# A macaron block on one core: PSUM as four pairs of banks instead of two double and four single places

## The chip, the cores and the metric

The kernel runs on one core of one Trainium2 chip. The metric is device time in microseconds (us) of one execution. A core has five engines with instruction queues of their own: TensorE (PE) multiplies matrices and writes only to PSUM; VectorE (DVE) and ScalarE (ACT) read PSUM and compute on rows; GpSimd (POOL) computes on SBUF alone; SyncE (SP) issues transfers. Each queue is worked off in order, and engines wait for each other through semaphores. PSUM has eight banks of 128 partitions by 512 fp32 values. One matmul writes into one bank.

## The reference

The input is x, 32 sequences of 256 tokens by 128 channels, in fp32. Three residual steps follow each other:

```
x = x + 0.5 * ffn(layernorm(x))          # weights L0_ffn_*
x = x + channel_attention(layernorm(x))  # weights L0_attn_W*
x = x + 0.5 * ffn(layernorm(x))          # the same weights as the first
```

`ffn` is a small transformer of two layers. Each layer shifts half of the channels by one token, projects to q, k and v for 8 heads of 64, normalizes q and k to length one, applies a scaled rotary embedding, and attends within windows of 64 tokens, looking back one window:

```
q, k, v = split(shift_token(x) @ wqkv, 3)
q, k = rotary_xpos(l2norm(q) * qs, l2norm(k) * ksc)
x = x + local_attention(q, k, v) @ wo
h = layernorm(shift_token(x)) * lg + lb
a, g = split(h @ w1 + b1, 2)
x = x + (a * gelu(g)) @ w2 + b2
```

`channel_attention` attends over channels instead of tokens, with 16 heads of 8 channels, so its score matrix is 128 by 128 for a sequence.

## The kernel before, in words

A sequence is two tiles of 128 tokens. For each of the 32 sequences the program builds a list of steps: load (SP), `ffn`, `channel_attention`, `ffn`, store. A step is a `plan.op`: the engines that may run it, a cost in us written out by hand, the function that emits its instructions, the steps it comes after, and the places it uses. A place is a buffer that a step takes from a list of a kind ("hT", "qk", "pT" and so on in SBUF) and gives back when its last user is done.

PSUM has two kinds of places: two "wide" ones of two banks each, and four "bank" ones of one bank (lines 112 and 113). Wide places hold the q and k projection (`project`, L197, two matmuls of 512 columns), the scores (`scores`, mask at L247 and 32 small products at L255) and the attended values (`attended`, L289, 32 small products). Bank places hold everything else: the value projection (L231), transposes of four or two 128-column blocks (`transposed`, L140, and `shifted_T`, L178), the output projection (L312), the hidden layer in three chunks (L381), its second matrix (L414) and the products of the channel attention (L458, L470, L496). Whatever lies in PSUM is read by ACT or DVE: copies (`evac`, L130, ACT unless DVE would end more than 1 us earlier), squares (L203), rotary products (L205 and L208), maximum and difference of the scores (L261 and L264), division (L296 and L297), GELU (L389), gated product (L396) and the residual sums (L317, L422, L501). GpSimd adds and scales q and k (L222 and L225), and computes the inverse norms (L124).

The order of all engines' work is fixed when the program is built. `Plan.order` simulates the engines with the costs of the steps, for up to eight sequences in flight. `begin` gives the earliest start of a step: when its inputs are there, its engine is free and each kind it lacks has a place, at the time at which that place was given back, plus a few hundredths of a us for a semaphore. `choose` picks the engine, `go` issues the step that can begin first, and takes the place that was given back longest ago. Every 15 TensorE steps the planner tries 16 orders of the next 60, with random delays, and keeps the one that ends first on TensorE. Its result is the order in which the steps' functions are called.

The framework below it then derives the semaphore waits from this order and from the tiles and slices that each instruction reads and writes. The planner does not see them.

Of the kernel before, what the change touches and what calls it, by code (L numbers as in the profile page):

```python
# [8 lines left out]
F32 = mybir.dt.float32  # L9
# [6 lines left out]
P = 128  # L16
# [24 lines left out]
def kernel(ctx: ExitStack, tc: tile.TileContext, ins: dict, out: bass.AP):  # L41
# [6 lines left out]
    psum = ctx.enter_context(tc.tile_pool(name="psum", bufs=2, space=PSUM))  # L48
# [30 lines left out]
    plan = Plan()  # L79

    for kind, n, shape in (
# [27 lines left out]
        ("v1", 12, [P, NT]),  # L109
    ):  # L110
        plan.places(kind, [hold.tile(shape, F32, name=f"{kind}{i}") for i in range(n)])
    for kind, n, shape in (("wide", 2, [P, 2, 512]), ("bank", 4, [P, 512])):
        plan.places(kind, [psum.tile(shape, F32, tag=f"{kind}{i}", name=f"ps_{kind}{i}", bufs=1) for i in range(n)])
    plan.places("sequence", range(CHAINS))

    for t in plan.free["vt"]:
# [531 lines left out]
class Plan:  # L648
# [16 lines left out]
    class Place:  # L665
        def __init__(self, kind):
            self.kind, self.t, self.users = kind, None, 0
# [2 lines left out]
        pass  # L670

    def __init__(self):
        self.free, self.ops, self.rank, self.base = {}, [], 0, 0

    def places(self, kind, tiles):
        self.free[kind] = list(tiles)
# [81 lines left out]
    def lacks(self, o):  # L758
# [4 lines left out]
                need[p.kind] = need.get(p.kind, 0) + 1  # L763
        return need

    def begin(self, o, engine):

        t = max(o.given[engine], self.clock[engine], self.clock["POOL"] if o.apart else 0.0)
        sync = self.SYNC[engine]
        for p in o.uses:  # L770
            if p.last and p.last[1] != engine and p.kind in self.TURNS:
                t = max(t, p.last[0] + sync)
        for k, n in self.lacks(o).items():
            if len(self.room[k]) < n:
                return None
            t = max(t, (min(self.since[k]) if n == 1 else sorted(self.since[k])[n - 1]) + sync)
        return t

    def choose(self, o):


        choice = None
        for engine, us in zip(o.engines, o.us):
            t = self.begin(o, engine)
            if t is None:
                return None
            load = self.TABLE * (engine == "ACT" and o.table not in (None, self.table))
            end = t + us + load + (self.RATHER if engine != o.engines[0] else 0.0)
            if choice is None or end < choice[0]:
                choice = (end, engine, t, us + load, t + load)  # L790
        return choice[1:]

    def go(self, until, later, chance):


        import heapq

        heap, barred = [], {}

        def push(o, t):  # L800
            heapq.heappush(heap, (round((t + later[o]) / self.ALIKE), o.key, o))

        def enter(o):
            if o not in later:
                later[o] = chance()
            push(o, min(o.given.values()))

        for o in self.ready:
            enter(o)
        while heap and (until is None or self.through < until):  # L810
            first, _, o = heapq.heappop(heap)
            choice = self.choose(o)
            if choice is None:
                barred.setdefault(next(k for k, n in self.lacks(o).items() if len(self.room[k]) < n), []).append(o)
                continue

            engine, t, us, rank = choice
            if round((rank + later[o]) / self.ALIKE) > first:
                push(o, rank)
                continue  # L820
            taken = []
            for p in o.uses:
                self.undo.append((p, dict(p.__dict__)))
                if p.t is None:
                    i = min(range(len(self.room[p.kind])), key=lambda i: self.since[p.kind][i])
                    p.t = self.room[p.kind].pop(i)
                    self.since[p.kind].pop(i)
                    taken.append((p, p.t))
                    for d in barred.pop(p.kind, []):
                        enter(d)  # L830
            self.out.append((o, engine, taken))
            self.clock[engine] = t + us
            if o.apart:
                self.clock["POOL"] = t + us
            self.through += engine == "PE"
            self.undo.append((o, {"done": None}))
            o.done = (t + us + o.late + self.TAIL[engine], engine)
            if engine == "ACT" and o.table not in (None, self.table):
                self.table = o.table
                waiting = [h[2] for h in heap]  # L840
                heap.clear()
                for d in waiting:
                    enter(d)
            for p in o.uses:
                p.left -= 1
                p.end, p.last = max(p.end, o.done[0]), o.done
                if not p.left:
                    self.room[p.kind].append(p.t)
                    self.since[p.kind].append(p.end)
                    for d in barred.pop(p.kind, []):  # L850
                        enter(d)
            for d in o.then:
                self.undo.append((d, {"wait": d.wait}))
                d.wait -= 1
                if not d.wait:
                    d.given = {
                        e: max(x.done[0] + (self.SYNC[e] if x.done[1] != e or x.late else 0.03) for x in d.after)
                        for e in d.engines
                    }
                    enter(d)  # L860
        self.ready = [h[2] for h in heap] + [o for os in barred.values() for o in os]
        return bool(heap) or not self.ready
# [48 lines left out]
```

## Time and profile before

| | |
|---|---|
| median of 3 runs | 2841.89 us (2840.95 to 2842.41) |
| the profiled execution's own time | 2842.17 us |
| its span, from the first instruction to the last | 2840.1 us |
| TensorE matmuls (PE) | 2788.2 us busy, 98% |
| TensorE weight loads (PEld) | 2114.4 us, 74% |
| VectorE (DVE) | 2135.1 us, 75% |
| ScalarE (ACT) | 1993.7 us, 70% |
| GpSimd (POOL) | 2302.2 us, 81% |
| granted TensorE clock, mean | 0.997 |

A group of instructions in the profile is one line, engine, operation and tile; after the bar stand its busy time in us, the mean time of one in ns, and the idle time of its engine just before it with what ended most of it. A line of the waits reads: engine, tile and line that waited, what ended the wait, us in total, number of waits, the longest. In the timeline stand start and length in us. A busy PE is not a PE at its peak: records of matmuls overlap, and their ends are modelled. Helpers share lines: every PSUM copy is L130, every transpose through `transposed` L140.

### The profile page before, as it was taken

How to read it: one execution, taken by the hardware profiler on the slowest of the kernel's cores; microseconds unless marked ns; L12 is line 12 of the kernel's file. 1: busy time of each engine (PE TensorE's matmuls, PEld its weight loads, DVE VectorE, ACT ScalarE, POOL GpSimd, SP SyncE). 2: the span in 40 equal slices, each digit the busy share in tenths (PEclk: the TensorE clock that was granted, in tenths of full speed). 3: DMA queues.
4: the chain of work that ended last, by engine and by line, in shares of the span. 5: the costliest groups of instructions: out<-in, count | busy, mean ns of one | idle time of the engine just before them, and what ended most of it. 6: DMA issues, size and time to landing. Idle time of an engine off the chain costs nothing.

```text
span 2840.1 us, 106723 instructions
## 1 busy us (share of the span) xinstructions
PE 2788.2 (98%) x46200; PEld 2114.4 (74%) x46200; DVE 2135.1 (75%) x3764; ACT 1993.7 (70%) x3601; POOL 2302.2 (81%) x2098
## 2 busy tenths in 40 slices
PE   7999999999999999999999999999999999999999
PEld 4777777777777777777777777777777777777677
DVE  5778778778777778677777777877787777777776
ACT  4776776767677776767777776776767677776675
POOL 8988879698889778787798878878788788875975
PEclk9999999999999999999999999999999999999999
DMA  3111121111211111111112112111121111110211
GB/s 109 31 46 44 38 52 47 39 51 37 55 38 47 46 40 48 38 49 45 44 51 53 46 36 52 46 36 47 47 55 47 37 46 44 43 46 20 53 42 41
DMA packets 125726, 129.82 MB, mean 46 GB/s; under 512 B 56606, under 2 KB 75592, under 8 KB 125256
## 3 DMA queue, kind: packets, MB, share of 16 engines
q1 hardware_dynamic: 124440, 122.60, 16.5%
q8 instruction: 363, 5.95, 0.9%
q14 instruction: 107, 0.88, 0.1%
q10 hardware_dynamic: 816, 0.39, 0.0%
HBM read 8.13 MB, written 4.19 MB: 4 GB/s over the span
## 4 chain that ended last, share of the span: by engine, by line
PE 86%; DVE 6%; ACT 3%; POOL 3%; issue 1%; DMA 1%; SPq 0%; ACTq 0%; DVEq 0%; POOLq 0%
PE ps_bank L140 20%; PE ps_wide L197 14%; PE ps_bank L381 11%; PE ps_wide L289 9%; PE ps_bank L312 8%; PE ps_wide L255 7%; PE ps_bank L231 7%; PE ps_bank L414 6%; PE ps_wide L247 3%; PE ps_bank L458 1%; PE ps_bank L178 1%; DVE qk L205 1%; DVE sq L208 1%; ACT sq L203 1%; POOL rn L124 1%
## 5 line engine op out<-in xcount | busy, mean ns | idle before, releaser
L124 POOL TENSOR_TENSOR rn<-ssq,mhalf 128x16 f32<-128x16 f32 x256 | 748.3, 2923 | 21.3
L222 POOL TENSOR_TENSOR qk<-qk,sq 128x1024 f32<-128x1024 f32 x256 | 606.4, 2370 | 163.8 <-DVE sq L208 83.4
L225 POOL TENSOR_TENSOR qk<-qk,rn 128x1024 f32<-128x1024 f32 x256 | 487.7, 1908 | 10.4
L197 PE MATMUL ps_wide<-wqkv,hT 128*128 128x512 f32 x1024 | 489.2, 600 | 2.0 <-ACT hT L130 1.2
L205 DVE TENSOR_TENSOR qk<-ps_wide,tab 128x1024 f32<-128x1024 f32 x256 | 312.2, 1219 | 184.7 <-ACT sq L203 101.7
L381 PE MATMUL ps_bank<-zT,w 128*128 128x256 f32 (+1 forms) x1536 | 379.3, 383 | 2.8 <-DVE zT L130 1.7
L203 ACT ACTIVATE sq<-ps_wide 128x1024 f32<-128x1024 f32 x256 | 262.5, 1025 | 154.2 <-PE ps_wide L197 91.6
L208 DVE TENSOR_TENSOR sq<-ps_wide,tab 128x1024 f32<-128x1024 f32 x256 | 311.4, 1217 | 66.8 <-ACT sq L203 32.6
L130 ACT COPY pT<-ps_bank 96x512 f32<-96x512 f32 x505 | 283.3, 584 | 101.1 <-PE ps_bank L140 98.7
L214 DVE TENSOR_REDUCE ssq<-sq 128x16 f32<-128x1024 f32 x256 | 310.0, 1211 | 57.2 <-ACT sq L203 56.4
L381 PEld LDWEIGHTS ps_bank<-zT,w 128*128 128x128 f32 (+1 forms) x1536 | 257.8, 178 | 70.8 <-issue 15.0
L140 PE MATMUL ps_bank<-ident,pr 128*96 128x128 f32 x2048 | 290.2, 275 | 5.1 <-ACT pr L267 2.4
L140 PE MATMUL ps_bank<-ident,qk 128*128 128x128 f32 x2048 | 290.8, 276 | 3.1 <-POOL qk L225 2.4
L261 DVE TENSOR_REDUCE mx<-ps_wide 128x8 f32<-128x768 f32 x256 | 242.9, 949 | 62.8 <-PE ps_wide L255 61.7
L197 PEld LDWEIGHTS ps_wide<-wqkv,hT 128*128 128x128 f32 x1024 | 179.4, 191 | 145.7 <-issue 133.3
L289 PE MATMUL ps_wide<-vt,pT 96*32 96x65 f32 x8192 | 282.1, 221 | 3.5 <-ACT pT L130 1.4
L289 PE MATMUL ps_wide<-vm,pT 96*32 96x65 f32 x8192 | 283.9, 221 | 1.5 <-DVE sq L208 0.7
L312 PE MATMUL ps_bank<-wo,oT 128*128 128x128 f32 x2048 | 275.9, 279 | 2.7 <-ACT oT L130 1.0
L140 PEld LDWEIGHTS ps_bank<-ident,qk 128*128 128x128 f32 x2048 | 236.4, 141 | 48.1 <-issue 24.0
L312 PEld LDWEIGHTS ps_bank<-wo,oT 128*128 128x128 f32 x2048 | 251.2, 191 | 27.1 <-issue 10.3
L140 PEld LDWEIGHTS ps_bank<-ident,pr 128*96 128x96 f32 x2048 | 225.1, 126 | 60.7 <-issue 29.3
L289 PEld LDWEIGHTS ps_wide<-vt,pT 96*32 96x32 f32 x8192 | 240.6, 109 | 37.8 <-issue 17.6
(101 smaller groups left out, 5430.1 us busy)
## 6 DMA issues: line engine op xcount, KB each, us to landing
vm<-vt SPq DMA_DIRECT2D x256, 195.0 KB
vm<-vt SPq DMA_DIRECT2D x256, 130.0 KB
vm<-vt SPq DMA_DIRECT2D x256, 65.0 KB
y<-y SPq DMA_DIRECT2D x128, 56.0 KB
x<-in_x SPq DMA_DIRECT2D x32, 128.0 KB
out<-x SPq DMA_DIRECT2D x32, 128.0 KB
y<-y SPq DMA_DIRECT2D x128, 7.5 KB
y<-y SPq DMA_DIRECT2D x128, 0.2 KB
```

The costliest lines, as they stand in the source:

```text
L124: nc.gpsimd.tensor_tensor(dst, src, mhalf[:, :n], ALU.pow)
L140: nc.tensor.transpose(pt.t[:rows, j * P : (j + 1) * P], src, ident)
L197: nc.tensor.matmul(wide.t[:, a], lhsT(), wqkv[:, l, a * INNER : (a + 1) * INNER], start=True, stop=True)
L203: "ACT", 0.92, lambda e: nc.scalar.activation(sq.t, pq(), AF.Square), [m], [wide, sq]
L205: c = plan.op("DVE", 1.14, lambda e: nc.vector.tensor_mul(qk.t, pq(), cos), [m] + made["tables"][l], [wide, qk])
L208: lambda e: nc.vector.tensor_mul(sn.t.rearrange(five, x=2), pq().rearrange(five, x=2)[:, :, :, ::-1, :], sin.rearrange(five, x=2)),
L214: "DVE", 1.13, lambda e: nc.vector.tensor_reduce(ssq.t, sq.t, AX.X, ALU.add), [s], [sq, ssq]
L222: f = plan.op("POOL", 2.42, lambda e: nc.gpsimd.tensor_add(qk.t, qk.t, sn.t), [c, i], [qk, sn])
L225: lambda e: nc.gpsimd.tensor_mul(qk.t, qk.t, rn.t.unsqueeze(3).to_broadcast([P, 2, HEADS, DH])),
L289: nc.tensor.matmul(o()[q, r, j, :], pTs[r].t[:FR, j, q], v[:, 2 * j + r, :], start=True, stop=True)
L312: nc.tensor.matmul(pw.t[:, :P], oT.t[:, j, :], wo[:, l, j, :], start=j == 0, stop=j == PAIRS - 1)
L381: nc.tensor.matmul(pa.t[:w, i * SEQ : (i + 1) * SEQ], w1[:, l, i * HID + c0 : i * HID + c0 + w], zf(), start=True, stop=True,)
```

## The change

The two kinds of PSUM places become one pool. There are four tiles of two banks each, the pairs. The kind "bank" now lists eight entries, a pair's number and a half (0 or 1). A step that needs a "wide" place takes both halves of a pair, which must both be free (`whole`). A step that needs a "bank" takes one half, of the pair's tile a slice (`grab`): first by the time at which it could start there, then by how few free halves its pair has, so that a half beside a used one comes first, then by the time at which it was given back. `give` puts a half or both back. `begin` lets a wide place start when the later of a pair's two halves was given back. The rest of the kernel is unchanged, though its line numbers after the pools are one higher.

```diff
-    for kind, n, shape in (("wide", 2, [P, 2, 512]), ("bank", 4, [P, 512])):
-        plan.places(kind, [psum.tile(shape, F32, tag=f"{kind}{i}", name=f"ps_{kind}{i}", bufs=1) for i in range(n)])
+
+    plan.pairs = [psum.tile([P, 2, 512], F32, tag=f"pair{i}", name=f"ps_{i}", bufs=1) for i in range(4)]
+    plan.places("bank", [(i, h) for i in range(4) for h in range(2)])
...
+    def whole(self):
+
+        since = {}
+        for (i, _), t in zip(self.room["bank"], self.since["bank"]):
+            since.setdefault(i, []).append(t)
+        return [(max(ts), i) for i, ts in since.items() if len(ts) == 2]
+
     def begin(self, o, engine):
...
         for k, n in self.lacks(o).items():
+            if k == "wide":
+                whole = self.whole()
+                if not whole:
+                    return None
+                t = max(t, min(whole)[0] + sync)
+                continue
             if len(self.room[k]) < n:
                 return None
...
+    def grab(self, p, t):
+
+        room, since = self.room, self.since
+        if p.kind == "wide":
+            i = min(self.whole())[1]
+            for h in range(2):
+                n = room["bank"].index((i, h))
+                room["bank"].pop(n), since["bank"].pop(n)
+            p.t, p.bank = self.pairs[i], i
+            return
+        pick = lambda n: since[p.kind][n]
+        if p.kind == "bank":
+            here = [i for i, _ in room["bank"]]
+            pick = lambda n: (max(since["bank"][n] + self.SYNC["PE"], t), here.count(here[n]), since["bank"][n])
+        n = min(range(len(room[p.kind])), key=pick)
+        p.t = p.bank = room[p.kind].pop(n)
+        since[p.kind].pop(n)
+        if p.kind == "bank":
+            p.t = self.pairs[p.bank[0]][:, p.bank[1], :]
+
+    def give(self, p):
+
+        if p.kind not in ("wide", "bank"):
+            self.room[p.kind].append(p.t)
+            self.since[p.kind].append(p.end)
+            return (p.kind,)
+        self.room["bank"] += [(p.bank, 0), (p.bank, 1)] if p.kind == "wide" else [p.bank]
+        self.since["bank"] += [p.end] * (2 if p.kind == "wide" else 1)
+        return "wide", "bank"
...
-                    i = min(range(len(self.room[p.kind])), key=lambda i: self.since[p.kind][i])
-                    p.t = self.room[p.kind].pop(i)
-                    self.since[p.kind].pop(i)
+                    self.grab(p, t)
...
-                    self.room[p.kind].append(p.t)
-                    self.since[p.kind].append(p.end)
-                    for d in barred.pop(p.kind, []):
+                    for d in [d for k in self.give(p) for d in barred.pop(k, [])]:
                         enter(d)
```

More of the change, by code (lines that the diff above doesn't have):

```diff
@@ L672, in __init__ @@
     def __init__(self):
-        self.free, self.ops, self.rank, self.base = {}, [], 0, 0
+        self.free, self.ops, self.rank, self.base, self.pairs = {}, [], 0, 0, []
     def places(self, kind, tiles):
@@ L813, in go @@
             if choice is None:
-                barred.setdefault(next(k for k, n in self.lacks(o).items() if len(self.room[k]) < n), []).append(o)
+                lacks = self.lacks(o).items()
+                kind = next((k for k, n in lacks if k != "wide" and len(self.room[k]) < n), "wide")
+                barred.setdefault(kind, []).append(o)
                 continue
```

## The prediction

> **What bounds the kernel now.** I read the page first, then the groups with their shapes kept apart, then the waits, then a stretch of the timeline, and last the order in which the built programs' instructions stand and what each waits for. The page:
>
> ```profile
> span 2840.1 us, 106723 instructions
> ...
> PE 2788.2 (98%) x46200; PEld 2114.4 (74%) x46200; DVE 2135.1 (75%) x3764; ACT 1993.7 (70%) x3601; POOL 2302.2 (81%) x2098
> ...
> PE 86%; DVE 6%; ACT 3%; POOL 3%; issue 1%; DMA 1%; SPq 0%; ACTq 0%; DVEq 0%; POOLq 0%
> ```
>
> TensorE is busy for 98% and is 86% of the chain that ended last, so its order of work sets the end; the others have room, but not much: 70 to 81%. A busy TensorE still hides short pauses, because a matmul's record overlaps the next one's. I therefore measured the 3586 groups of matmuls that the planner places (one `plan.op` each) by the distance from a group's first start to the next group's. The tenth percentile of a kind is its bare width: 0.436 us for four transposes (L140), 0.858 for a value projection (L231), 0.863 for a hidden chunk (L381), 0.891 (L312), 1.338 (L414), 1.717 (L197), 1.345 (L247 and L255), 1.047 (L289). Widths times counts give 2684.2 us; 9.6 lie before the first matmul and 5.3 after the last group's start; the remaining 141.1 of the span are pauses. Of these 66.2 are pauses under 0.115 us, mostly a step that recurs whatever is waited for. The other 169 hold 74.9: in 35.8 the input came last, in 25.6 the reader that frees the PSUM place, in 13.5 nothing that the trace tells. In 115 of them, 55.4 us, the last releaser is ACT or DVE; 45.4 of that lies after the first 100 us.
>
> So what PSUM's border can cost today is 25.6 us, 0.9%. Next, how closely the readers of PSUM follow TensorE:
>
> ```profile
> ACT pT L130 <- PE ps_bank L140: 98.7, 117, 5.5
> ACT oT L130 <- PE ps_bank L140: 97.2, 87, 3.6
> ...
> ACT vt L130 <- PE ps_bank L231: 78.2, 124, 3.0
> ```
>
> ```profile
> L140 PE MATMUL ps_bank<-ident,pr 128*96 128x128 f32 x2048 | 290.2, 275 | 5.1 <-ACT pr L267 2.4 <-ACT pT L130 0.9 <-DVE y L422 0.6
> ...
> L130 ACT COPY pT<-ps_bank 96x512 f32<-96x512 f32 x505 | 283.3, 584 | 101.1 <-PE ps_bank L140 98.7 <-ACT zT L130 0.6 <-ACT z L163 0.3
> ```
>
> ```profile
> 1405.31 1.04 PE L140 MATMUL ps_bank<-ident,pr 128*96 128x128 f32 x8
> ...
> 1406.01 1.07 ACT L130 COPY pT<-ps_bank 96x512 f32<-96x512 f32 x2
> ```
>
> The eight transposes are two groups in two banks. The copy of the first starts at 1406.01 while the second group still runs until 1406.35. Over all ACT copies of L130 the median start is 0.119 us after the end of the group that fed them: they are rarely late because of their own queue. The nearest later use by TensorE (of the copied tile or the freed bank) follows the copy's end by 0.086 us at the 5th percentile, 0.224 at the 10th, 1.226 at the median.
>
> **The change, part by part.** *The pool.* Two double tiles and four single ones become four double tiles; eight banks before and after, nothing to time. *The planner's choice* (`whole`, `grab`, `give`, `begin`): up to four double places or eight single ones, and a single one goes first to a pair whose other half is used. It adds no instruction of its own, but every engine's order changes. TensorE keeps the same 3586 groups of the same kinds, so its 2684 us of widths stay. Copies on DVE rise from 34 to 51 (17 x 0.69 us = 12 us more on DVE, 17 x 0.586 = 10 us less on ACT) and table loads fall from 178 to 164 (14 x 1.283 = 18 us less on ACT); with 700 us idle on each, both are hidden, and 0. SP's 1235 transfers remain, and the lookups of the planner run at build time.
>
> *The waits.* This part decides. In the built program of before, every read of PSUM waits for exactly the group that filled its bank, and every TensorE wait on a reader is for that group's own bank. In the changed program a pair acts in part as one place:
> - 1187 reads (722 ACT copies, 149 GELUs, 316 on DVE) wait for a later group, one that writes the *other* half; in 987 it is the very next group.
> - 547 TensorE waits are for a reader of the other half.
> - 481 reads on ACT or DVE wait for the other engine's read of the other half, where no matmul waited for that already.
>
> The planner's `begin` knows none of these, so it plans starts that will not happen; and its preference for the used pair puts the next group just where the wait arises. Queued behind a late copy on ACT are the next copies, squares and exponentials; TensorE waits for the tiles.
>
> *Their price.* The delay of one read is at most the width of the neighbour's group. The widths of the 1187 add up to 723.6 us (231 of L140 on `qk`, 194 on `pr`, 104 on `ob`, at 0.436 each; 208 of L381 at 0.863; 113 of L231; 103 of L312; the rest smaller). Taking off what the reads lag anyway, by the lags of the same lines in the trace of before, about 359 us of delay stay, most on ACT's 846 us of idle time. What reaches TensorE I count from the order. Lay the groups end to end by their widths. A reader starts at the earliest 0.205 us after the last group it waits for leaves the issue slot (0.167 is a transpose's record less its slot, 0.276 - 0.109; 0.038 the shortest lag), takes its row's mean, and must end 0.055 before the group that needs it (the shortest slack in the trace). Before it on its queue stand k instructions that may be late in the same way. Where it can't be done, the rest is a shortfall; of those that overlap the largest alone counts. All together (groups, us):
> - before: k=0 42, 14.8; k=1 97, 27.2; k=2 134, 38.3; k=3 158, 50.9.
> - after: k=0 169, 94.9; k=1 310, 151.1; k=2 374, 188.9; k=3 404, 221.8.
>
> The trace's own 45.4 us (past the start, which loads set) lie 0.56 of the way from k=2 to k=3. The differences there are 150.6 and 170.9; at 0.56 that is 162. Bounds: 80.1 (k=0: no queue behind a late read), less the 25.6 of PSUM waits if all of them went, +54.5; above, 170.9 scaled by 55.4/50.9 is 186, and the 481 cross-engine waits, which the count leaves out, may add half a copy (0.3 us) each at the share of short hand-offs (404 in 3586, 11%): 16, or 202. The freer choice of places brings nothing that I can count: without the reads' new waits k=2 would be no looser than before.
>
> *A rule that says otherwise.* The Trainium skill, "Perfetto Trace Analysis", section Optimizing Tensor Performance, has independent groups rotate through banks so that the evacuation of one overlaps the next group. The timeline above shows it: 1406.01 against 1406.35. By the rule a neighbour bank is as good as any other, the new waits cost 0, and the best is 2841.9 - 25.6 = 2816. The chip doesn't ask for them ("PSUM — Partial Sum Buffer", section on bank collisions: different banks ran clean; no run here tries it), but the program has them, and an engine obeys its program. I take the program.
>
> **Sum.** The profiled execution took 2842.17 us, its span 2840.1 and 2.1 around it; the median of the runs, 2841.89, is 0.3 below it. Span 2840.1 + 162 = 3002, and with the 2.1 less 0.3 around it: 3004 us.
>
> **The rivals.**
> - *Likeliest, 2896 to 3080, 3004:* the waits across the halves stall TensorE. 0.80.
> - *Absorbed:* lateness passes into slack (median 1.2 us) and each pause gives the following reads time, leaving a third of k=2, 50 us: 2848 to 2896. The 700 us of idle on ACT speak for it; the 5th percentile of slack, 0.086 us against delays of 0.436, against. 0.08.
> - *Faster, the other side:* the 25.6 us go, with some input waits, since a double tile may take any of four pairs: 2816. It decides only if fewer than about 26 us of the new waits arrive, a third of the k=0 count, which has no queue in it. 0.04.
> - *It does nothing measurable,* 2836 to 2848, gain and loss cancel. 0.02.
> - *Collapse:* late reads set POOL back too (81% busy, and its L222 waits for DVE), and all engines lose their overlap: over 3080. 0.06.
>
> **How the numbers follow.** 0.2% (5.7 us) is what a measurement of this kernel can tell from no change. Slower: 0.80 + 0.08 + 0.06 = 0.94; same 0.02; faster 0.04. The range runs from 2890, just under the lower bound, to 3080, 36 above the upper one for what the count omits; it leaves out about 0.19.
>
> **What the changed profile would show.** Right: 46200 matmuls again with idle on TensorE up from 52 to some 150 us or more and its busy share near 94 to 96%; TensorE's list of waits led by ACT copies and DVE reads in tenfold amounts; on ACT larger totals of pT, qT, vt and oT copies waiting for a PE line that is not the one that fills them. Wrong: TensorE still at 98% with PSUM waits gone (the rule), or pauses ended by POOL or DMA (another cause). The forecast fails if the hardware's lags are longer than their percentiles in ways that hide the delay, or if the count's overlapping rule is too generous.

## The result, and the profile after

The changed kernel takes 3054.78 us (median of 4 runs, 3050.27 to 3058.15) against 2842.15 (4 runs, 2840.95 to 2843.90) of the kernel before: a ratio of 1.0744, interval 1.0731 to 1.0757. It is slower by 212.6 us; 3004 had been forecast, in a range of 2890 to 3080. The profiled execution took 3058.15 us, 1.75 more than its span.

The page of the changed kernel, with the lines that answer those shown of before (the span; the engines' busy time; the chain that ended last, by engine):

```profile
span 3056.4 us, 106603 instructions
...
PE 2856.6 (93%) x46200; PEld 2118.6 (69%) x46200; DVE 2158.2 (71%) x3781; ACT 1967.0 (64%) x3570; POOL 2300.2 (75%) x2098
...
PE 61%; ACT 9%; DVE 6%; issue 3%; POOL 1%; DMA 1%; SPq 0%; ACTq 0%; DVEq 0%; POOLq 0%
```

TensorE has the same 46200 records of matmuls (a product of fp32 values leaves two, a transpose one), but 200 us of its span are idle (3056.4 - 2856.6), where 52 were. ACT, DVE and POOL do the same work within 27 us, so no engine has become the bound: all of them wait more. In the chain, ACT's share rises from 3 to 9% and TensorE's falls from 86 to 61%. The shares named add up to 81% only, so the size of the loss is better read from the starts of the groups of matmuls, as in the prediction. Its groups have the same widths, 2684.2 us in all. (They are 3554 steps of the planner in either kernel; the prediction's 3586 counts one step of the channel attention, which has two lines, as two groups. The sums are the same either way.) Their pauses grew from 141.1 to 356.5:

| pauses between groups, us | before | after |
|---|---|---|
| up to 0.115 us each | 66.2 | 68.1 |
| longer, the input came last | 35.8 | 92.6 (172 pauses) |
| longer, the reader of the PSUM place came last | 25.6 | 152.3 (248) |
| longer, nothing that the trace tells | 13.5 | 43.5 (99) |

Of the 216.3 us by which the span grew, 213.5 are in the longer pauses. The small step that recurs at every group stayed what it was.

What the copies on ACT waited for, in the list of waits after the change (us in total, number, longest):

```profile
ACT pT L131 <- PE ps L141: 67.6, 85, 3.2
...
ACT oT L131 <- PE ps L141: 52.0, 44, 5.3
ACT vt L131 <- PE ps L232: 50.9, 42, 3.1
...
ACT vt L131 <- PE ps L141: 23.0, 24, 3.3
...
ACT pT L131 <- DVE y L318: 16.4, 15, 3.4
...
ACT vt L131 <- PE ps L382: 13.6, 12, 3.3
ACT gg L390 <- PE ps L141: 13.3, 23, 2.2
...
ACT pT L131 <- PE ps L313: 11.0, 17, 1.5
```

A "vt" tile is filled by L232 alone, "gg" by L382, "pT" and "oT" by L141. The vt rows show the change most clearly: the waits on L232 fell from 78.2 to 50.9 us, and 23.0 us of waits on transposes and 13.6 on the hidden layer, which have nothing to do with the copied data, took their place. The first row, pT on L141, is a mixture, because a transpose can also be the neighbour: of the 185 copies into pT that in the built program wait for a neighbour's group, 120 wait for transposes. "DVE y L318" in the same list is a read on another engine: the copy waits for DVE to finish reading the other half. The two groups that the prediction showed, with shapes kept apart (busy, mean ns, idle before it and what ended most of that):

```profile
L141 PE MATMUL ps<-ident,pr 128*96 128x128 f32 x2048 | 289.0, 276 | 24.9 <-ACT pr L268 6.5
...
L131 ACT COPY pT<-ps 96x512 f32<-96x512 f32 x503 | 282.1, 585 | 128.6 <-PE ps L141 67.6 <-DVE y L318 16.4 <-PE ps L313 11.0
```

One transpose takes 276 ns (275 before) and one copy 585 (584); only the idle time in front of them changed, from 5.1 to 24.9 us and from 101.1 to 128.6. And on TensorE's side, the waits after the change:

```profile
PE ps L313 <- ACT oT L131: 9.4, 19, 1.1
PE ps L141 <- ACT gg L390: 9.1, 16, 1.4
PE ps L382 <- ACT zT L131: 7.9, 17, 1.0
```

The first of these was, before:

```profile
PE ps_bank L312 <- ACT oT L130: 1.0, 4, 0.3
```

A transpose waiting for a GELU (L390), which it has nothing to do with, did not occur before. Apart from a row that is mostly one wait of 9.5 us near the start (11.1 us, 14.9 before) no row of the list reaches 10 us: the loss is spread over many short waits.

One place in the timeline of the changed kernel shows the mechanism (start, length, engine, what runs, idle before it and what ended it):

```profile
1447.81 1.02 ACT L204 ACTIVATE sq<-ps 128x1024 f32<-128x1024 f32 x1
...
1447.94 0.64 PE L141 MATMUL ps<-ident,pr 128*96 128x128 f32 x4 [0.18 <-ACT vt L131]
...
1448.42 1.06 PE L313 MATMUL ps<-wo,oT 128*128 128x128 f32 x8
...
1449.52 0.58 ACT L131 COPY pT<-ps 96x512 f32<-96x512 f32 x1 [0.69 <-PE ps L313]
```

The four transposes that fill the copy's bank end at 1448.58, and ACT is free from 1448.83. The copy starts at 1449.52, just after the matmuls of L313 have ended (1449.48; four of fp32, eight records), which in the built program write the other half of the same pair. ACT stood idle for 0.69 us with its data ready. Over all copies of L131 the median start was 0.119 us after the end of the group that fed them before the change, and is 0.574 after it.

### The profile page after: what moved, and what is told of

It reads as the page before. It is cut to its first block, busy times and chain, and to the rows that moved or that the text cites. A ratio compares the mean times of both kernels' runs of the same rounds, so it can differ in the third digit from the quotient of the medians.

```text
span 3056.4 us, 106603 instructions
## 1 busy us (share of the span) xinstructions
PE 2856.6 (93%) x46200; PEld 2118.6 (69%) x46200; DVE 2158.2 (71%) x3781; ACT 1967.0 (64%) x3570; POOL 2300.2 (75%) x2098
## 3 DMA queue, kind: packets, MB, share of 16 engines
q1 hardware_dynamic: 124440, 122.60, 15.3%
## 4 chain that ended last, share of the span: by engine, by line
PE 61%; ACT 9%; DVE 6%; issue 3%; POOL 1%; DMA 1%; SPq 0%; ACTq 0%; DVEq 0%; POOLq 0%
PE ps L141 13%; PE ps L198 10%; PE ps L382 8%; PE ps L313 6%; PE ps L290 6%; PE ps L256 5%; PE ps L232 5%; PE ps L415 4%; PE ps L248 2%; ACT pT L131 1%; ACT gg L390 1%; PE ps L459 1%; DVE sq L209 1%; DVE uT L397 1%; DVE qk L206 1%
## 5 line engine op out<-in xcount | busy, mean ns | idle before, releaser
L198 PE MATMUL ps<-wqkv,hT 128*128 128x512 f32 x1024 | 494.4, 605 | 3.9 <-DVE hT L131 1.5
L206 DVE TENSOR_TENSOR qk<-ps,tab 128x1024 f32<-128x1024 f32 x256 | 311.9, 1218 | 142.2 <-ACT sq L204 95.2
L382 PE MATMUL ps<-zT,w 128*128 128x256 f32 (+1 forms) x1536 | 386.7, 387 | 20.6 <-ACT zT L131 7.9
L131 ACT COPY pT<-ps 96x512 f32<-96x512 f32 x503 | 282.1, 585 | 128.6 <-PE ps L141 67.6
L209 DVE TENSOR_TENSOR sq<-ps,tab 128x1024 f32<-128x1024 f32 x256 | 311.1, 1216 | 37.6 <-PE ps L198 21.4
L382 PEld LDWEIGHTS ps<-zT,w 128*128 128x128 f32 (+1 forms) x1536 | 258.3, 179 | 101.6 <-ACT zT L131 17.5
L141 PE MATMUL ps<-ident,pr 128*96 128x128 f32 x2048 | 289.0, 276 | 24.9 <-ACT pr L268 6.5
L141 PE MATMUL ps<-ident,qk 128*128 128x128 f32 x2048 | 289.6, 276 | 21.5 <-POOL qk L226 4.2
L313 PE MATMUL ps<-wo,oT 128*128 128x128 f32 x2048 | 278.4, 280 | 17.3 <-ACT oT L131 9.4
L290 PE MATMUL ps<-vm,pT 96*32 96x65 f32 x8192 | 284.8, 221 | 8.8 <-issue 3.8
L313 PEld LDWEIGHTS ps<-wo,oT 128*128 128x128 f32 x2048 | 251.0, 191 | 54.6 <-ACT oT L131 21.8
L290 PE MATMUL ps<-vt,pT 96*32 96x65 f32 x8192 | 282.8, 221 | 5.5 <-issue 1.7
L141 PEld LDWEIGHTS ps<-ident,qk 128*128 128x128 f32 x2048 | 234.6, 141 | 69.3 <-issue 35.3
L141 PEld LDWEIGHTS ps<-ident,pr 128*96 128x96 f32 x2048 | 224.3, 127 | 79.1 <-issue 17.9
```

The source lines that it names most:

```text
L131: lambda e: (nc.scalar.copy if e == "ACT" else nc.vector.tensor_copy)(dst(), src()), after, uses,
L141: nc.tensor.transpose(pt.t[:rows, j * P : (j + 1) * P], src, ident)
L198: nc.tensor.matmul(wide.t[:, a], lhsT(), wqkv[:, l, a * INNER : (a + 1) * INNER], start=True, stop=True)
L206: c = plan.op("DVE", 1.14, lambda e: nc.vector.tensor_mul(qk.t, pq(), cos), [m] + made["tables"][l], [wide, qk])
L209: lambda e: nc.vector.tensor_mul(sn.t.rearrange(five, x=2), pq().rearrange(five, x=2)[:, :, :, ::-1, :], sin.rearrange(five, x=2)),
L290: nc.tensor.matmul(o()[q, r, j, :], pTs[r].t[:FR, j, q], v[:, 2 * j + r, :], start=True, stop=True)
```

## The experiments

The theory is that of the prediction: the waits across the two halves of a pair, which the program asks for and the planner doesn't know, make up the loss. Three kinds of them can be taken apart: *reads* that wait for matmuls into the other half, *TensorE* waiting for a reader of the other half, and *turns*, a read on ACT or DVE that waits for the other's read of the other half. The rivals: the new order of the work, or the new choice of places, costs the time by itself; or the preference for a bank beside a used one does, because it puts the next group where the wait arises.

A wait is taken away by telling the framework that two instructions on different engines are independent if they touch different halves of a pair and share no other tile. The edit, here for all three kinds:

```diff
+    APART = ("wait", "read", "turn")
+    def note(self, tc, engine, made):
...
+                for j, e, h, o, r in past:
+                    kind = "wait" if engine == "PE" else "read" if e == "PE" else "turn"
+                    shared = {n for n in o & (out | read) | r & out if not n.startswith("ps_")}
+                    if e != engine and not h & halves and not shared and kind in self.APART:
+                        tc.declare_no_dep(i, j, query=mybir.DependencyQuery.ANY, reason="other half")
...
             o.fn(engine)
+            self.note(tc, engine, all[n:])
```

All results first. The difference is to the kernel before, run beside it on the same chip.

| kernel | us | ratio, interval | difference |
|---|---|---|---|
| the changed kernel | 3054.78 | 1.0744, 1.0731 to 1.0757 | +212.6 |
| its order, no waits across halves | 2834.85 | 0.9968, 0.9957 to 0.9980 | -9.2 |
| before's order and border, banks as halves of pairs | 3162.92 | 1.1121, 1.1106 to 1.1136 | +318.8 |
| changed, without the reads' waits | 2883.98 | 1.0140, 1.0126 to 1.0154 | +39.9 |
| changed, without TensorE's waits | 3000.13 | 1.0547, 1.0531 to 1.0563 | +156.0 |
| changed, without the turns | 3024.39 | 1.0639, 1.0624 to 1.0653 | +182.1 |
| changed, without the preference | 3039.49 | 1.0691, 1.0676 to 1.0705 | +197.2 |
| changed, the planner told of the waits | 2869.24 | 1.0092, 1.0079 to 1.0106 | +26.9 |
| no waits, no preference | 2829.26 | 0.9954, 0.9940 to 0.9968 | -13.0 |
| before's order and border, halves, no waits | 2843.23 | 1.0000, 0.9991 to 1.0008 | 0.0 |
| no waits, preference turned round | 2840.47 | 0.9992, 0.9983 to 1.0001 | -2.7 |

### The changed kernel's order, without any wait across halves

The edit is the one above; the order of every engine's work and the places in PSUM stay those of the changed kernel.

> The changed kernel with its own order of work on every engine, but with all waits across the two halves of a pair taken out: each bank waits for its own users alone. Theory (the waits across halves make the loss): 2838 us, within 2815 to 2860; by the count of shortfalls the order alone is 3.5 us looser than that of before. Rival (the planner's new order is the worse one, the waits hardly matter): over 2950. Rival (freer places are worth their 25.6 us once nothing hinders them): 2816 or less.

Measured: 2834.85 us, ratio 0.9968. The whole loss is gone, and 9 us with it. Its page:

```profile
span 2835.7 us, 106819 instructions
...
PE 2777.7 (98%) x46200; PEld 2120.2 (75%) x46200; DVE 2146.5 (76%) x3781; ACT 1956.6 (69%) x3570; POOL 2300.2 (81%) x2098
```

TensorE is back at 98%. The same place in its timeline, with the same three steps:

```profile
1345.43 0.60 PE L141 MATMUL ps<-ident,pr 128*96 128x128 f32 x4
...
1345.63 1.02 ACT L204 ACTIVATE sq<-ps 128x1024 f32<-128x1024 f32 x1 [0.15 <-PE ps L198]
...
1345.86 1.06 PE L313 MATMUL ps<-wo,oT 128*128 128x128 f32 x8
...
1346.55 0.57 ACT L131 COPY pT<-ps 96x512 f32<-96x512 f32 x1
```

The copy starts at 1346.55, about when ACT is done with the squares, while L313 writes the other half until 1346.92. And the waits of ACT's copies are on the matmuls that fill them again:

```profile
ACT pT L131 <- PE ps L141: 82.0, 103, 2.8
...
ACT vt L131 <- PE ps L232: 76.9, 111, 3.8
```

So neither the new order nor the new choice of places costs time.

### The old order and border, with the single banks as halves of pairs

```diff
-    for kind, n, shape in (("wide", 2, [P, 2, 512]), ("bank", 4, [P, 512])):
-        plan.places(kind, [psum.tile(shape, F32, tag=f"{kind}{i}", name=f"ps_{kind}{i}", bufs=1) for i in range(n)])
+    pairs = [psum.tile([P, 2, 512], F32, tag=f"pair{i}", name=f"ps_{i}", bufs=1) for i in range(4)]
+    plan.places("wide", pairs[:2])
+    plan.places("bank", [pairs[i][:, h, :] for i in (2, 3) for h in range(2)])
```

This is an edit of the kernel before. The planner is that of before and gives the same order; only the four single tiles are now two double ones. In the built program 919 reads come to wait for a neighbour's group, TensorE waits 1274 times for a reader of the other half, and there are 871 turns (in this wider count of turns the changed kernel has 745; the prediction's 481 leaves out those beside a matmul's wait).

> The kernel before with its own order and its fixed border, but the four single banks are halves of two double tiles, so only the waits across halves are new (1274 on TensorE, 919 reads behind a neighbour's matmuls, 871 between ACT and DVE). Theory: slower by what the count of shortfalls gives, 306 - 45 = 261 us: 3103, within 2980 to 3200, although nothing moved. Rival (the new order makes the loss): 2842 to 2860.

Measured: 3162.92 us, 318.8 more than before. This is the loss without the change: no pool, no new choice, only tiles that span two banks. The page's line of the engines and TensorE's own list of waits:

```profile
PE 2901.5 (92%) x46200; PEld 2110.2 (67%) x46200; DVE 2149.1 (68%) x3764; ACT 2013.2 (64%) x3601; POOL 2300.9 (73%) x2098
```

```profile
PE ps L141 <- ACT pT L131: 22.2, 44, 1.3
PE ps L141 <- DVE uT L397: 15.4, 24, 1.6
PE ps L141 <- ACT vt L131: 12.1, 25, 0.9
```

Pauses whose last releaser is a reader of PSUM hold 276.7 us here, 25.6 before. The loss is larger than the changed kernel's; that all the groups that need one bank share two pairs here, and four there, would explain it, but was not tried apart. It is not the number of late reads, which is smaller here (919 against 1187).

### The same with the waits taken away

The kernel of the last experiment, with the function `note` of the first:

```diff
+    APART = ("wait", "read", "turn")
...
+            self.note(tc, engine, all[n:])
```

> Control for the way in which waits are taken out: the kernel before, its four single banks as halves of two double tiles as in the run at 3163, with all waits across halves out again. Theory (these waits are all that the shared tile adds): 2842, within 2836 to 2850. Rival (slices of a double tile cost something else, an address or a bank): above 2860.

Measured: 2843.23 us over 12 runs, ratio 1.0000 (0.9991 to 1.0008). Taking the waits away gives back the time of the kernel before, to within 0.1%, so neither the double tiles nor the edit cost or save anything else, and the 318.8 us above are the waits alone.

### One kind of wait at a time

The first experiment's edit on the changed kernel, with one name in its list, here the reads:

```diff
-    APART = ("wait", "read", "turn")
+    APART = ("read",)
```

Reads no longer wait for the neighbour's matmuls; the other two kinds stay:

> The changed kernel, in which only the reads of ACT and DVE no longer wait for the neighbour's matmuls; TensorE still waits for the neighbour's readers, and ACT and DVE for each other. Theory (the late reads are the larger part): by the count 67 - 45 = 22 us over before, 2864, with the turns between ACT and DVE up to 2900. Rival (TensorE's own new waits are the larger part): over 2980.

TensorE no longer waits for readers of the other half:

> The changed kernel, in which only TensorE no longer waits for readers of the other half. Theory (late reads are the larger part): by the count 167 - 45 = 121 us over before, 2963, with the turns up to 3010. Rival (TensorE's own waits are the larger part): under 2920.

ACT and DVE no longer wait for each other's reads of the other half:

> The changed kernel, in which only ACT and DVE no longer wait for each other's read of the other half (745 waits). The prediction allowed this kind 16 us and left it out of its sum; with the late reads gone and all else gone 49 us were still between 2884 and 2835, shared with TensorE's waits. Theory (a small part): 3055 less 5 to 25, so 3030 to 3050. Rival (the kind that the count left out explains why it came out 50 us low): 2995 to 3010.

Measured: 2883.98, 3000.13 and 3024.39 us. Against the changed kernel's +212.6 the reads are worth 172.7 us (212.6 - 39.9), TensorE's waits 56.6, the turns 30.5. The three add up to 259.8, more than the 221.8 that go when all go together (212.6 + 9.2), so the kinds are not independent: part of the time needs two of them at once. The reads are the largest by a factor of three, and the copies' lag behind their own group follows them: with the reads' waits out its median is 0.163 us, against 0.574 in the changed kernel and 0.139 with no waits at all. The copies into vt wait for their own matmuls again:

```profile
ACT vt L131 <- PE ps L232: 81.5, 110, 3.7
```

The turns missed what was expected of them: 3024.39 lies below the 3030 to 3050 of the theory and above the 3010 of the rival. They are more than a small part and do not explain the missing 50 us alone.

### Without the preference for a used pair

```diff
-            pick = lambda n: (max(since["bank"][n] + self.SYNC["PE"], t), here.count(here[n]), since["bank"][n])
+            pick = lambda n: since["bank"][n]
```

The waits stay; the bank given back longest ago is taken, whatever lies beside it.

> The changed kernel, in which a single bank is taken by the time at which it was given back alone, as before the change, not beside a used one first. Pairs and waits across halves stay. The count of shortfalls is 202 us against 45 of before; at the 1.3 that the measured losses of the changed kernel and of the two others show over their counts: 3045, within 3000 to 3090. Rival (the preference puts the next group into the wait, so without it most of the loss is gone): under 2950.

Measured: 3039.49 us, 15.3 less than the changed kernel. The count of shortfalls had said much the same: 202 us for this order, against 207 for the changed kernel reckoned in the same way (0.56 of the way from 188.9 to 221.8). As the main cause the preference falls.

### The planner told of the waits

```diff
+        self.touch = {i: {} for i in range(4)}
...
+            if p.t is not None and p.kind in self.TURNS:
+                t = max(t, self.others(self.pair(p), engine))
...
+            if k == "bank":
+                t = max(t, min(max(s + sync, self.others(b[0], engine)) for b, s in zip(self.room[k], self.since[k])))
...
-            pick = lambda n: (max(since["bank"][n] + self.SYNC["PE"], t), here.count(here[n]), since["bank"][n])
+            pick = lambda n: (max(since["bank"][n] + self.SYNC["PE"], self.others(here[n], "PE"), t), here.count(here[n]), since["bank"][n])
```

`touch` keeps, for each pair and engine, the end of its last step there; `others` is the time at which the last step of another engine on that pair ends. All waits stay in the program; the planner only counts with them when it places the steps.

> The changed kernel, with the planner told of the waits: a step on a pair can begin only when the last steps of the other engines on either half are over, and a bank is taken by that. The waits themselves stay in the program. Theory (waits that nobody planned for make most of the loss; planned ones can be worked around): count of shortfalls 67 us, 21 over before, times 1.3: 2870, within 2850 to 2910. Rival (the waits cost the same however the work is ordered): over 3000.

Measured: 2869.24 us, 26.9 over the kernel before. It loses an eighth as much as the changed kernel. Its program still has 784 reads behind a neighbour's group, where the changed kernel has 1187; TensorE's waits for a reader of the other half and the turns, counted in one way from the two built programs, are 594 against 587 and 513 against 689. Its page and two of its waits:

```profile
PE 2787.8 (97%) x46200; PEld 2115.3 (74%) x46200; DVE 2149.4 (75%) x3757; ACT 1959.6 (68%) x3588; POOL 2300.2 (80%) x2098
```

```profile
ACT vt L131 <- PE ps L232: 47.7, 48, 3.6
...
ACT vt L131 <- PE ps L382: 7.6, 9, 1.2
```

Copies still wait for matmuls that don't feed them, and they start as late as in the changed kernel: 0.569 us after the end of their own group in the median, against 0.574. That there are fewer such reads is not enough to explain the gain either, for the old order with pairs has 919 of them, a median of 0.519, and loses 318.8 us. So what cost 185.7 us (212.6 - 26.9) is mainly that the waits were not planned for. How much of it the planner saves by another order of the work and how much by another choice of banks was not tried apart.

### The free pool with the waits away: three choices of the place

Without any waits across halves, the pool itself can be judged. With the preference it is the first experiment (2834.85). Without it:

```diff
+    APART = ("wait", "read", "turn")
...
-            pick = lambda n: (max(since["bank"][n] + self.SYNC["PE"], t), here.count(here[n]), since["bank"][n])
+            pick = lambda n: since["bank"][n]
```

> As the run with all waits across halves taken out, and without the preference for a bank beside a used one. The preference's one use is then to keep whole pairs free for double places. Theory of that use: 2840 to 2855, slower than the 2835 with it. Rival (it matters no more): 2830 to 2840.

With the preference turned round, a bank of a wholly free pair first:

```diff
+    APART = ("wait", "read", "turn")
...
-            pick = lambda n: (max(since["bank"][n] + self.SYNC["PE"], t), here.count(here[n]), since["bank"][n])
+            pick = lambda n: (max(since["bank"][n] + self.SYNC["PE"], t), -here.count(here[n]), since["bank"][n])
```

> All waits across halves out, and the preference turned round: a bank of a wholly free pair first. Theory (packing or not matters little when banks are independent): 2830 to 2850; the count of shortfalls is 49, 4 over before. Rival (whole pairs run short, double places wait): over 2860.

Measured: 2829.26 us (0.9954, 0.9940 to 0.9968) and 2840.47 (0.9992, 0.9983 to 1.0001). Without any preference the free pool is 0.46% faster than the kernel before, and the fastest kernel here. With the preference turned round the gain can't be told from no change. The first of the two ran against its expectation: without the preference the double places were thought to run short (2840 to 2855), and the kernel came out below even the rival's 2830 to 2840. A pool without a border is therefore worth a little, and choosing a wholly free pair first gives it up. Whether the preference for a used pair gives up a part as well is not shown: its interval (0.9957 to 0.9980) overlaps that of the kernel without it. The span of the fastest kernel is 13.8 us shorter than before's, its pauses hold 10.4 us less, but those that a reader of PSUM ends only 3.0 less (22.6 against 25.6). Where the rest of the gain comes from is not shown; the order of all the work is another one.

## Why the prediction was right, and where it was off

*The bound and the widths.* Right: the groups' widths are 2684.2 us in both kernels, and 213.5 of the 216.3 us are longer pauses. Nothing in the engines' own work had to be counted: the shifts of copies from ACT to DVE and of table loads were hidden, as costed.

*The waits decide, and the program's waits are obeyed.* Right, and shown from both sides: with after's order and no such waits 2834.85 us, with before's order and only such waits 3162.92, and back to 2843.23 when they are taken out again. One would not expect these waits from the description of the kernel before, by which they follow from tiles and slices: two halves of a PSUM tile are different slices, and the built programs order them all the same. The rule that the prediction set against the trace (the Trainium skill, "Perfetto Trace Analysis", Optimizing Tensor Performance: rotate groups through banks) would have given 2816. Its overlap comes once the banks are independent for the program: in the first experiment a copy reads one half while matmuls fill the other, and TensorE is at 98%. The time is still 2834.85 and not 2816, because the PSUM waits did not go away (see below). For two halves of one tile between which the program has waits, the overlap doesn't come.

*The size.* 162 us were forecast, 212.6 came. The step that failed is the sum's treatment of the turns: they were left out of it and allowed 16 us at most, by half a copy at the share of short hand-offs, for 481 of them. Taken away alone they are worth 30.5; that edit takes out 745, for it also takes those beside which a matmul's wait stands. The count of shortfalls, for which the turns don't exist, is tested by the kernel without turns: it forecasts 162, and 182.1 was measured, 11% too little (20 of 182). So of the 50 us that are missing, about 30 are the turns and about 20 the count, which takes only the largest of overlapping shortfalls and no lateness beyond three queued instructions. Which of these two simplifications costs the 20 us was not tried. The split holds with the other waits left in; as the kinds share part of their time, it could come out otherwise in another order of removal. With turns and all, the same count was low by much the same share elsewhere: 261 us for 318.8 measured (old order, pairs), 121 for 156.0 (without TensorE's waits), 157 for 197.2 (without the preference), 21 for 26.9 (the planner told). The upper bound of 202 that the prediction derived was too low by 11 us; the 36 us of margin above it held the result.

*The preference.* Misjudged: the prediction had it put the next group "just where the wait arises". It does, but its share is 15 us of 213. That the planner doesn't know the waits was the other half of the sentence, and it is the one that counts: with a planner that is told of them the loss is 26.9.

*The freedom of places.* "Nothing that I can count" was close, but not quite nothing: 9 us with the preference, 13 without, both more than the 0.2% that can be told from no change; the 25.6 us of PSUM waits that were taken as its bound did not go away (20.5 and 22.6 stayed).

*The rivals.* Absorption into slack is refuted for the changed kernel: a loss of 50 us was its number. The nearest to it is the kernel whose planner knows the waits: its copies start as late, and 26.9 us are lost. But there the order was made for it; here slack that was there by chance did not do it. The collapse through POOL did not come: POOL's busy time stayed at 2300 us, and the transposes that take POOL's results waited 4.2 us for them, 2.4 before.

*The signs named in advance.* TensorE idle for 200 us (150 or more had been said) but busy for 93%, a point below the 94 to 96 named, as the loss was larger; copies that wait for a line that doesn't fill them, as said, for oT too: such waits rose from nothing to 25.5 us, though its idle time in all fell from 100.7 to 91.2; ninefold for oT on TensorE's list, but many rows instead of a few leaders, and at its head the same wait near the start as before.

## What to carry to other kernels

Before memory that engines share is pooled, count what the built program will wait for, tile by tile: if waits are recorded for a whole tile, its two halves are one place, whatever the hardware allows. A planner that doesn't model such waits can pay dearly for them, while one that does can hide most of the cost: here 212.6 us against 26.9, with copies that start equally late. And a pool is better judged with such waits out: free of them, this one was worth 13 us, which was invisible under a loss of 213.

## What the hardware showed

Reading one half of a pair while TensorE fills the other cost nothing that can be measured. In the first experiment, by the trace and the built program's banks together, 121 of ACT's copies into pT ran while matmuls wrote the other half of the same pair for more than half of the copy's time. Their median is 582 ns, against 584 for 329 copies with nothing written into their pair. The other way round, 426 transposes ran wholly while ACT read the other half; they took 275 ns in the mean, those without such a read 277. With all waits across halves away, the kernel with double tiles and the one with single tiles differ by 0.0% (1.0000, 0.9991 to 1.0008). The prediction left this untried with the Trainium skill, "PSUM — Partial Sum Buffer", section on bank collisions, where accesses of two engines to different banks ran clean. That speaks of errors, not of time; the time is what these runs add. Reads of one bank beside matmuls into another were there before the change too, as the prediction's own timeline shows.

Less expected was how little the lateness of the copies says by itself. In the changed kernel they start 0.455 us later in the median (0.574 - 0.119), which is less than one copy takes, on an engine that is idle for a third of the time; yet the pauses on TensorE grew by 215 us. With the planner told they start as late, and 26.9 us are lost.
